# The tail of a fused attention and density kernel: four endings moved to GpSimd, and one term of each sum written to PSUM by ScalarE

## The chip, the cores and the metric

The kernel runs on one core of a Trainium2 chip. Its engines are TensorE (PE in the profile), VectorE (DVE), ScalarE (ACT), GpSimd (POOL) and SyncE (SP, which issues DMAs). Each takes its own instructions in the order in which they were written and waits on semaphores for the others. The metric is the device time of one execution in microseconds.

## What is computed

The input has 8 images of 192 channels and 64 x 64 positions, in float32. After a group norm and an attention over positions, whose result is added to the input, comes a second group norm and a small per-channel network of four layers (1-3-3-3-1), evaluated at the normalized value minus and plus one half:

```
lower = _logits_cumulative(xr - 0.5, ms, bs, fs)
upper = _logits_cumulative(xr + 0.5, ms, bs, fs)
sign = -jnp.sign(lower + upper)
likelihood = jnp.abs(sigmoid(sign * upper) - sigmoid(sign * lower))
x = x + jnp.maximum(likelihood, 1e-06)
```

Each layer is `logits = softplus(m) @ logits + b`, and all but the last add `tanh(f) * tanh(logits)`. The network is called the density below.

## The kernel before

**Stages.** The attention of the 8 images runs as one stream of 1,024 steps. An image's density needs the norm over all of its attention output, so it runs beside the attention of the next image; that of the last image has nothing beside it and is the tail of the kernel.

**Units.** A density is cut into 12 units (`Unit`, L908): two column halves c, three channel groups g, and s = 0, 1 for lower and upper, in that order. A unit works on 128 x 1024 tiles, and a pair s = 0, 1 is followed by an `ending` (L1173). In the tail a unit goes thus:

- three tanh of the input on ACT (`tanh0`, L1015), called u;
- three sums of layer 1 on PE (`product`, L983), each four terms: one in x and three in the u, with diagonal matrices as weights and two matmuls of 512 columns per term, added up in one of four PSUM tiles (`banks`: b0, b1, sc_tail, mx_tail[...]). `tanh1` (L996, ACT) and `gate1` (L1006, DVE) read the sum, and the gate gives the tile back;
- layer 2: three rows, each a scaled copy on ACT (`scaled`, L1040) and two additions on DVE (`more`), a tanh (`tanh`, L1030) and a gate (`gate`). `more` and `gate` are written by `stt`, L1047;
- layer 3: one scaled copy and two additions.

**Endings.** While attention runs, an ending is cut into half-tile pieces for POOL (`total`, `difference`, `masked`, L1195 to L1218), with the tanh and the sign on ACT (L1202, L1204); ahead of each piece a small memset (`pause`, L1163) waits for the last DVE operation but one, so that the piece falls beside the reduce that reads PSUM. In the tail an ending is `alone` (L1220): sum (L1227), difference (L1239) and mask (L1240) on DVE, two whole tanh on ACT (L1233). Both close with an Abs on ACT (L1249) and a `store` on DVE (L1254) with two DMAs. Units of earlier images also leave two pieces each for POOL (`plain`, L1072 and L1078).

**What sets the order.** The program writes its instructions in ticks. In each, `density_step` (L1120) gives every engine a credit, and units (up to four in the tail) issue their next operations while credit lasts, at the costs of `COST` (L866), if their inputs were issued in an earlier tick, a PSUM tile is free and enough of the 17 buffers are left for older units (`need`, L1094). Other work is put on a list by tick (`at`, `later`). In the tail the rate is `RATE` = 4.15 (L1426). `pool_step` (L1158) issues one piece per tick.

Of the kernel before, what the change touches and what calls it, by code (L numbers as in the profile page):

```python
# [10 lines left out]
AF = mybir.ActivationFunctionType  # L11
# [6 lines left out]
def kernel(  # L18
# [43 lines left out]
    nc = tc.nc  # L62

    B, C, H, W = x.shape
# [12 lines left out]
    last = B * IMG  # L77
# [40 lines left out]
    for i in range(3):  # L118
        t = xin.tile([128, 3, P], F32, tag=f"xi{i}", name=f"xi{i}")
# [58 lines left out]
    for i in range(2):  # L178
        nc.vector.tensor_reduce(
            out=bb[i], in_=ident[:, 64 * i + CR : 64 * i + 64 : 32], axis=AX.X, op=ALU.add  # L180
# [6 lines left out]
    for s in range(2):  # L187
        p = slice(R * s, R * s + R)
# [45 lines left out]
    for src, dst, at, n in (  # L234
# [4 lines left out]
        for s in range(2):  # L239
            nc.sync.dma_start(  # L240
                out=dst[R * s : R * s + R, :, at : at + n],
# [85 lines left out]
    now = [0]  # L327
# [538 lines left out]
    COST = {"DVE": 1.22, "ACT": 1.23, "TANH": 1.05, "PE": 6.95}  # L866
    diag = []
    banks = deque()
    lower2 = mm.rearrange("p g n -> p (g n)")[:, 0:36].rearrange("p (s g i) -> p s g i", s=4, g=3)

    def diagonals(g, t):
# [36 lines left out]
    class Unit:  # L908
# [3 lines left out]
        def __init__(self, b, c, g, s):  # L912
            self.key = b, c, g, s
            self.at = {}
            self.buf = {}
            self.todo = {"DVE": deque(), "ACT": deque(), "PE": deque()}
            self.left = {"l": 6, "t": 9, "u": 0, "z": 1, "p": 1}
            self.held = {"l": 0, "t": 0, "u": 0, "z": 0, "p": 0}
            self.on_pe = b == B - 1
            add = self.add  # L920
            if self.on_pe:

                self.left.update(t=3, u=3, p=0)
                for i in range(3):
                    add("ACT", ("u", 0, i), [], self.tanh0, makes="u")
                for i in range(3):
                    add(
                        "PE", ("sum", i), [("u", 0, j) for j in range(3)], self.product,
                        frees=[("u", 0, j) for j in range(3)] if i == 2 else [],
                    )  # L930
                    add("ACT", ("l", 1, i), [("sum", i)], self.tanh1, makes="l")
                for i in range(3):
                    add("DVE", ("gate", 1, i), [("l", 1, i)], self.gate1)
            else:
                for i in range(3):
                    add("ACT", ("t", 0, i), [], self.tanh0, makes="t")
                    add("ACT", ("l", 1, i), [], self.linear, makes="l")
                for i in range(3):
                    for j in range(3):
                        add(  # L940
                            "DVE", ("mix", i, j), [("t", 0, j), ("l", 1, i)], self.mix,
                            frees=[("t", 0, j)] if i == 2 else [],
                        )
                    add("ACT", ("t", 1, i), [("mix", i, 2)], self.tanh, makes="t")
                for i in range(3):
                    add("DVE", ("gate", 1, i), [("t", 1, i)], self.gate, frees=[("t", 1, i)])
            for i in range(3):
                add("ACT", ("l", 2, i), [("gate", 1, 0)], self.scaled, makes="l")
                for j in (1, 2):
                    add("DVE", ("add", 2, i, j), [("gate", 1, j), ("l", 2, i)], self.more)  # L950
                add("ACT", ("t", 2, i), [("add", 2, i, 2)], self.tanh, makes="t")
            for i in range(3):
                add("DVE", ("gate", 2, i), [("t", 2, i)], self.gate, frees=[("t", 2, i)])
            add("ACT", ("l", 3, 0), [("gate", 2, 0)], self.scaled, makes="z")
            add("DVE", ("add", 3, 0, 1), [("gate", 2, 1), ("l", 3, 0)], self.more)
            if self.on_pe:
                add("DVE", ("add", 3, 0, 2), [("gate", 2, 2), ("l", 3, 0)], self.more)
            else:

                add("ACT", ("p", 3, 2), [("gate", 2, 2), ("add", 3, 0, 1)], self.plain, makes="p")  # L960

        def add(self, eng, name, after, fn, makes=None, frees=()):
            self.todo[eng].append((name, after, fn, makes, frees))
# [15 lines left out]
        def src(self):  # L979
            b, c, g, s = self.key  # L980
            return xc[b, c][:, g, :]

        def product(self, k):  # L983
            g, i = self.key[2], k[1]
            out = self.buf[k] = banks.popleft()
            for n, src in enumerate([self.src()] + [self.buf["u", 0, j] for j in range(3)]):
                for h in range(2):
                    nc.tensor.matmul(  # L988
                        out[:, h, :], lhsT=diag[g][:, 3 * i + n - 1 if n else 9 + i, :],
                        rhs=src[:, h * F : h * F + F], start=n == 0, stop=n == 3,  # L990
                    )

        def tanh1(self, k):
            b, c, g, s = self.key
# [6 lines left out]
        def gate1(self, k):  # L1001

            g, i = self.key[2], k[2]
            dst = self.buf["l", 1, i].rearrange("p (h n) -> p h n", h=2)
            src = self.buf.pop(("sum", i))
            nc.vector.scalar_tensor_tensor(  # L1006
                dst, dst, tf[:, g, 3 + i : 4 + i], src, ALU.mult, ALU.add
            )
            banks.append(src)

        def tanh0(self, k):
            b, c, g, s = self.key
# [81 lines left out]
        def need(self):  # L1094
            most = dict(self.left, t=max(0, min(self.left["t"], 1 - self.held["t"])))
            if ("add", 2, 2, 2) not in self.at:

                most.update(z=0, p=0)
            return sum(most.values())

        def step(self, eng, t, older):
            todo = self.todo[eng]
            while todo and credit[eng] > 0:
                name, after, fn, makes, frees = todo[0]
                if any(self.at.get(a, t) >= t for a in after if eng != "DVE" or a[0] in "ltu"):
                    return
                if eng == "PE" and not banks:
                    return
                if makes and len(bufs) <= sum(u.need() for u in older) + len(endings):
                    return  # L1110
                todo.popleft()
                if makes:
                    self.take(name, makes)
                fn(name)
                self.at[name] = t
                for k in frees:
                    self.give(k)
                credit[eng] -= COST["TANH" if name[0] == "t" and name[1] else eng]
# [39 lines left out]
    def pool_step():  # L1158


        if pieces:
            if len(recent) == 2:
                inst = nc.gpsimd.memset(pause, 0.0)  # L1163
                tc.add_manual_dep(
                    inst.ins, recent[0].ins.name,
                    mybir.DependencyInfo(
                        mybir.DependencyClass.Sync, mybir.DependencyReason.DATA
                    ),
                    reason="beside the reduce",
                )  # L1170
            pieces.popleft()()

    def ending(b, c, g):  # L1173

# [8 lines left out]
        def begin():  # L1183
            if not bufs:
                later(1, begin)
                return
            endings.pop()
            cell["s"] = bufs.pop(0)
            if now[0] < last - 12:
                for h in range(2):  # L1190
                    pieces.append(lambda h=h: total(h))
            else:
                alone()
# [26 lines left out]
        def alone():  # L1220

            s = cell["s"]
            parts = halves if (b, c, g) == (B - 1, 1, 2) else [slice(0, 2 * F)]

            def first():
                for n in parts:
                    nc.vector.tensor_tensor(s[:, n], z[0][:, n], z[1][:, n], ALU.add)  # L1227
                later(1, second, 0.0, 2.1)

            def second():  # L1230
                for n in parts:
                    for i in range(2):
                        nc.scalar.activation(z[i][:, n], z[i][:, n], AF.Tanh, scale=0.5)  # L1233
                later(1, third, 2.5)

            def third():
                for n in parts:
                    y = z[0][:, n]
                    nc.vector.tensor_tensor(y, z[1][:, n], y, ALU.subtract)  # L1239
                    nc.vector.scalar_tensor_tensor(y, s[:, n], 0.0, y, ALU.not_equal, ALU.mult)  # L1240
                bufs.extend((s, z[1]))
                later(1, lambda: size(parts), 0.0, 1.1)
                later(2, lambda: store(parts), 1.3)

            later(1, first, 1.25)
# [177 lines left out]
    homes[:] = [(turns[1], [0, 0])]  # L1423
    while due or units or jobs or loads:

        work_off(t, RATE if (B - 1, 1) in norms else 1.3)  # L1426
        t += 1
# [1 line left out]

# [36 lines left out]
```

## Time and profile before

| | |
|---|---|
| median of 3 runs | 4800.04 us (4797.65 to 4801.9) |
| the profiled execution | 4801.53 us |
| its span, first to last instruction | 4799.7 us |
| busy over the span | PE 97%, DVE 87%, ACT 67%, POOL 18% |
| in 4473 to 4527 us (54 us) | PE 34.37, DVE 51.23, ACT 35.47, POOL 9.05 us; clock 0.79 |
| in 4527 to 4588 us (61 us) | PE 56.06, DVE 45.60, ACT 37.69, POOL 0 us; clock 1.00 |
| a PE record of L988 | 592 ns, a new one every 0.43 us at full clock; two records per matmul |

Durations include the time in which an operation's end overlaps the start of the next one, so back-to-back starts are closer together than durations suggest: L1030 lasts 1.05 us and is followed 0.95 us later. "idle before <- releaser" in a timeline is how long the engine stood before the instruction, and what released it. A window row gives, for each engine, its busy time in that stretch and the number of instructions, and at the end the granted TensorE clock (1.00 is full speed).

### The profile page before, as it was taken

How to read it: one execution, taken by the hardware profiler on the slowest of the kernel's cores; microseconds unless marked ns; L12 is line 12 of the kernel's file. 1: busy time of each engine (PE TensorE's matmuls, PEld its weight loads, DVE VectorE, ACT ScalarE, POOL GpSimd, SP SyncE). 2: the span in 40 equal slices, each digit the busy share in tenths (PEclk: the TensorE clock that was granted, in tenths of full speed). 3: DMA queues.
4: the chain of work that ended last, by engine and by line, in shares of the span. 5: the costliest groups of instructions: out<-in, count | busy, mean ns of one | idle time of the engine just before them, and what ended most of it. 6: DMA issues, size and time to landing. Idle time of an engine off the chain costs nothing.

```text
span 4799.7 us, 69014 instructions
## 1 busy us (share of the span) xinstructions
PE 4653.4 (97%) x28432; PEld 3440.0 (72%) x28432; DVE 4179.0 (87%) x4289; ACT 3196.8 (67%) x3665; POOL 856.3 (18%) x842
## 2 busy tenths in 40 slices
PE   7999999999999999999999999999999999999686
PEld 5777777777777777777777777777777777777332
DVE  5433359999999999999999999999999999998788
ACT  2333246777677767776777767777777777777675
POOL 0000001222122211221211221122222132222000
PEclk9999999999999999999999999999999999999898
DMA  2101020111110111010110111101111101000000
GB/s 58 41 18 29 18 48 14 35 28 29 42 27 25 37 39 34 27 44 9 36 46 26 33 40 33 32 19 33 36 38 33 34 13 27 10 12 16 9 13 13
DMA packets 109328, 138.60 MB, mean 29 GB/s; under 512 B 17106, under 2 KB 82132, under 8 KB 109012
## 3 DMA queue, kind: packets, MB, share of 16 engines
q1 hardware_dynamic: 107776, 133.81, 11.4%
q8 instruction: 223, 3.65, 0.3%
q14 instruction: 93, 0.76, 0.1%
q10 hardware_dynamic: 1236, 0.37, 0.0%
HBM read 100.58 MB, written 29.36 MB: 27 GB/s over the span
## 4 chain that ended last, share of the span: by engine, by line
PE 86%; DVE 7%; ACT 5%; issue 1%; DMA 0%; POOL 0%; ACTq 0%; SPq 0%; DVEq 0%; POOLq 0%
PE b L795 53%; PE sc L780 20%; PE b L669 4%; DVE d L1047 4%; PE b L988 2%; PE b L620 2%; DVE rm L716 1%; ACT d L1015 1%; ACT e L784 1%; PE mx_tail L988 1%; PE sc_tail L988 1%; PE b L828 1%; PE mx L708 1%; ACT d L1040 1%; PE b L745 0%
## 5 line engine op out<-in xcount | busy, mean ns | idle before, releaser
L795 PEld LDWEIGHTS b<-v,e 128*128 128x128 f32 x16384 | 2651.8, 190 | 776.9 <-issue 771.6
L795 PE MATMUL b<-v,e 128*128 128x193 f32 x16384 | 2955.7, 334 | 0.0
L784 ACT ACTIVATE e<-sc 128x1024 f32<-128x1024 f32 x1024 | 1045.9, 1021 | 1353.4 <-PE mx L708 1330.8
L716 DVE TENSOR_REDUCE rm<-mx 128x1 f32<-128x1024 f32 x1002 | 1222.3, 1220 | 481.4 <-PE mx L708 472.7
L780 PE MATMUL sc<-q,k 25*128 25x512 f32 x4096 | 1155.1, 640 | 24.2 <-ACT e L784 22.9
L708 PE MATMUL mx<-k,q 24*128 24x512 f32 x4008 | 1130.4, 640 | 0.6 <-DVE rm L716 0.6
L1047 DVE SCALAR_TENSOR_TENSOR d<-d,lc,d 128x1024 f32<-128x1024 f32 x756 | 986.1, 1314 | 12.2
L1047 DVE SCALAR_TENSOR_TENSOR d<-d,wsp,d 128x1024 f32<-128x1024 f32 x684 | 883.3, 1292 | 53.1 <-ACT d L1040 44.7
L1047 DVE SCALAR_TENSOR_TENSOR d<-d,tf,d 128x1024 f32<-128x1024 f32 x540 | 687.5, 1292 | 0.4 <-ACT d L1030 0.4
L1163 POOL MEMSET pause<- 128x1 f32 x408 | 40.0, 98 | 3613.2 <-DVE d L1047 3613.2
L1030 ACT ACTIVATE d<-d 128x1024 f32<-128x1024 f32 x540 | 568.2, 1054 | 42.6 <-DVE d L1047 40.8
L780 PEld LDWEIGHTS sc<-q,k 25*128 25x128 f32 x4096 | 306.2, 183 | 252.4 <-issue 175.8
L1040 ACT ACTIVATE d<-d,cb,wsp 128x1024 f32<-128x1024 f32 x348 | 429.9, 1236 | 4.3 <-DVE d L1047 3.3
L1015 ACT ACTIVATE d<-xc,bn,wn 128x1024 f32<-128x1024 f32 x288 | 354.0, 1236 | 7.7 <-issue 5.9
L1078 POOL TENSOR_TENSOR d<-d,d 128x512 f32<-128x512 f32 x168 | 331.8, 1975 | 47.7 <-ACT d L1072 46.6
L1024 ACT ACTIVATE d<-xc,bn,wn 128x1024 f32<-128x1024 f32 x252 | 311.8, 1237 | 0.0
L708 PEld LDWEIGHTS mx<-k,q 24*128 24x128 f32 x4008 | 299.8, 183 | 7.3 <-DVE rm L716 6.7
L1198 POOL TENSOR_TENSOR d<-d,d 128x512 f32<-128x512 f32 x80 | 173.0, 2163 | 0.0
L1210 POOL TENSOR_TENSOR d<-d,d 128x512 f32<-128x512 f32 x80 | 163.2, 2040 | 0.5 <-issue 0.5
L1218 POOL TENSOR_TENSOR d<-d,d 128x512 f32<-128x512 f32 x80 | 157.6, 1970 | 2.5 <-POOL pause L1163 0.9
L669 PE MATMUL b<-wv,xi 64*128 64x192 f32 x1344 | 139.5, 340 | 0.0
L669 PEld LDWEIGHTS b<-wv,xi 64*128 64x128 f32 x1344 | 106.5, 186 | 25.4 <-issue 21.5
(155 smaller groups left out, 2303.9 us busy)
## 6 DMA issues: line engine op xcount, KB each, us to landing
xi<-in_x_dram SPq DMA_DIRECT2D x280, 192.0 KB, 3.5
xc<-in_x_dram SPq DMA_DIRECT2D x64, 384.0 KB, 7.1
out_dram<-xc SPq DMA_DIRECT2D x94, 256.0 KB, 3.1
q<-qd SPq DMA_DIRECT2D x128, 128.0 KB, 2.7
k<-kq SPq DMA_DIRECT2D x64, 64.0 KB, 1.9
qd<-kq SPq DMA_DIRECT2D x64, 64.0 KB, 2.0
d<-in_x_dram SPq DMA_DIRECT2D x16, 192.0 KB, 4.1
out_dram<-xc SPq DMA_DIRECT2D x4, 128.0 KB
```

The source lines that it names most:

```text
L669: nc.tensor.matmul(pv[:, s, 0:C], lhsT=t[p, g, k * 128 : k * 128 + 128] if g < 3 else one_row[p], rhs=wf["v", b][p, g, :] if g < 3 else wf ...
L708: nc.tensor.matmul(sc[:, s, :], lhsT=tile_of(qt[b, n // 2], n, j)[r], rhs=kt[b][r, u : u + F], start=True, stop=True,)
L716: nc.vector.tensor_reduce(out=rowmax[b, n][:, j, k : k + 1], in_=sc, axis=AX.XY, op=ALU.max)
L780: nc.tensor.matmul(sc[:, s, :], lhsT=kt[b][r, k : k + 128], rhs=qt[b, n // 2][r, :, u : u + 256], start=True, stop=True,)
L784: return lambda: nc.scalar.activation(e, sc, AF.Exp)
L795: nc.tensor.matmul(a[:, j, 0 : C + 1], lhsT=e[:, s, j * 128 : j * 128 + 128], rhs=v[:, s, p % 4, :], start=p == 0 and s == 0 and j % 2 == ...
L1015: nc.scalar.activation(self.buf[k], self.src(), AF.Tanh, bias=bn[:, s, g, 0, i : i + 1], scale=wn[:, g, 0, i : i + 1],)
L1024: nc.scalar.activation(self.buf[k], self.src(), AF.Identity, bias=bn[:, s, g, 1, i : i + 1], scale=wn[:, g, 1, i : i + 1],)
L1030: nc.scalar.activation(self.buf[k], self.buf["l", k[1], k[2]], AF.Tanh)
L1040: nc.scalar.activation(self.buf[k], self.buf["l", n - 1, 0], AF.Identity, bias=offset, scale=wsp[:, g, w : w + 1],)
L1047: nc.vector.scalar_tensor_tensor(dst, src, factor, dst, ALU.mult, ALU.add)
L1078: return nc.gpsimd.tensor_tensor(z[:, n], z[:, n], dst[:, n], ALU.add)
```

## The change

1. `fill`: for the second and third sum of a unit in the tail, ACT writes the term in x (a scaled copy of x) into the PSUM tile, if a product has been in that tile before (`full`). The product then leaves its two matmuls in x out and adds onto what is there. The tanh of a sum is written behind the next sum instead of behind its own.
2. Endings of the last image with 3c + g < 4, four of its six, are cut into POOL pieces. A piece is issued in `gate1`, with its pause waiting for the DVE operation before the gate; `pool_step` issues none while the oldest unit is one of the tail's.
3. Orders: the tail's rate is 2.5 for 4.15; a tail unit whose third sum is not yet issued reserves its missing u and four buffers more (`need`); an ending of an earlier image first issues the pieces that are left.

The core of the diff (line numbers of the changed kernel: fill L998, product L1014, `tanh1` L1025, `gate1` L1035, pause L1201):

```
                 for i in range(3):
+                    after = [("u", 0, j) for j in range(3)]
+                    if i:
+                        add("ACT", ("fill", i), [("sum", 0)], self.fill)
+                        after.append(("fill", i))
                     add(
-                        "PE", ("sum", i), [("u", 0, j) for j in range(3)], self.product,
+                        "PE", ("sum", i), after, self.product,
...
-                    add("ACT", ("l", 1, i), [("sum", i)], self.tanh1, makes="l")
+                    if i:
+                        add("ACT", ("l", 1, i - 1), [("sum", i - 1)], self.tanh1, makes="l")
+                add("ACT", ("l", 1, 2), [("sum", 2)], self.tanh1, makes="l")
...
+        def fill(self, k):
+            b, c, g, s = self.key
+            i = k[1]
+            if id(banks[0]) in full:
+                out = self.buf["sum", i] = banks.popleft()
+                nc.scalar.activation(
+                    out, self.src().rearrange("p (h n) -> p h n", h=2), AF.Copy,
+                    scale=norms[b, 1][0][:, g, 1, i : i + 1],
+                )
...
             for n, src in enumerate([self.src()] + [self.buf["u", 0, j] for j in range(3)]):
+                if n == 0 and filled:
+                    continue
...
+            if filled:
+                credit["PE"] += 1.7
...
-            nc.vector.scalar_tensor_tensor(
+            recent.append(nc.vector.scalar_tensor_tensor(
                 dst, dst, tf[:, g, 3 + i : 4 + i], src, ALU.mult, ALU.add
-            )
+            ))
             banks.append(src)
+            if pieces and len(recent) == 2:
+                piece()
...
+            if self.on_pe and ("sum", 2) not in self.at:
+                return most["u"] + 4
...
-        if pieces:
+        if pieces and not (units and units[0].on_pe):
+            piece()
...
-            if now[0] < last - 12:
+            if now[0] < last - 12 or b == B - 1 and 3 * c + g < 4:
...
             def first():
+                while pieces and b < B - 1:
+                    piece()
...
-        work_off(t, RATE if (B - 1, 1) in norms else 1.3)
+        work_off(t, 2.5 if (B - 1, 1) in norms else 1.3)
```

## What was predicted

> **What bounds the kernel.** I read the page's chain by line first, to find which part of it the change can touch.
>
> ```profile
> PE 86%; DVE 7%; ACT 5%; issue 1%; DMA 0%; POOL 0%; ACTq 0%; SPq 0%; DVEq 0%; POOLq 0%
> PE b L795 53%; PE sc L780 20%; PE b L669 4%; DVE d L1047 4%; PE b L988 2%; PE b L620 2%; DVE rm L716 1%; ACT d L1015 1%; ACT e L784 1%; PE mx_tail L988 1%; PE sc_tail L988 1%; PE b L828 1%; PE mx L708 1%; ACT d L1040 1%; PE b L745 0%
> ```
>
> The attention stages (L795, L780) keep their instructions. What changes begins at L988, the tail: the stretch from 4470 us, where the last image's density starts, to 4799.7. At most some 330 us are in play. Next the tail by windows, each from one unit's first layer-2 addition to that of the unit two later (a pair s=0,1 with its ending).
>
> ```profile
> core 0: us, PE busy (x) PEld busy (x) DVE busy (x) ACT busy (x) POOL busy (x), PEclk, DMA share, GB/s
> 4634.52:4679.81 45.29, 41.74 (x97) 18.07 (x96) 39.25 (x34) 31.25 (x30) 0.00 (x0) 1.00 0.05 12
> 4679.81:4725.10 45.29, 41.73 (x97) 18.07 (x96) 39.24 (x33) 31.25 (x30) 0.00 (x0) 1.00 0.05 12
> 4770.38:4799.70 29.32, 0.00 (x0) 0.00 (x0) 19.03 (x20) 10.12 (x12) 0.00 (x0) 0.52 0.08 18
> ```
>
> A pair takes 45.3 us; PE is busy for 41.7, DVE 39.25, ACT 31.25, POOL not at all. The last 29.3 us hold no product. The chain in such a pair:
>
> ```profile
> 4679.45 12.28 PE b L988 x28
> 4691.73 6.88 PE sc_tail L988 x16
> 4698.64 1.11 ACT d L996
> 4699.76 1.13 ACT d L1040
> 4700.88 1.14 ACT d L1015
> ```
>
> PE and its wait for the next unit's tanh set the pace. DVE's own waits, in its timeline:
>
> ```profile
> 4634.52 2.60 DVE L1047 SCALAR_TENSOR_TENSOR d<-d,wsp,d 128x1024 f32<-128x1024 f32 x2
> 4639.38 2.60 DVE L1047 SCALAR_TENSOR_TENSOR d<-d,wsp,d 128x1024 f32<-128x1024 f32 x2 [2.25 <-ACT d L1040]
> 4641.90 1.27 DVE L1006 SCALAR_TENSOR_TENSOR d<-d,tf,sc_tail 128x1024 f32<-128x1024 f32 x1
> 4644.24 2.60 DVE L1047 SCALAR_TENSOR_TENSOR d<-d,wsp,d 128x1024 f32<-128x1024 f32 x2 [1.07 <-ACT d L1040]
> ```
>
> From two additions to the next two is 4.85 us: ACT's next row product stands behind a tanh that needs the first two. It is a round trip, and no engine is full in it.
>
> **What the change takes and adds.** A product is 16 records of 0.43 us, 6.87. The order of the changed kernel has 22 fills (every second and third product but the first unit's, since a bank must have been written before), so PE sheds 4 records, 1.72 us, 22 times: 37.8 us, 6.9 of a pair's 41.7. ACT gains 22 fills. No ACT write into PSUM stands in the trace. Nearest are the scaled copy L1072 (1.13 us, SBUF to SBUF) and the PSUM-reading L996 (1.11); starts follow each other about 0.1 sooner, so 1.05. Ends: 0.95 and 1.24 (the two-pointer L1015). Two stand on a unit's path, so the ends are worth -0.2 and +0.4 a unit where nothing covers them, about -2 and +4 us over the tail.
>
> Four endings lose three DVE operations each (starts 1.14, 1.26 and 1.14 us apart: 3.54), 14.2 in all. POOL gains six half pieces and a pause per ending, ACT six half activations (0.63 us each by L1202 and L1204, 0.53 apart: 3.2) for two whole tanh (1.9): +1.3. The stores and their DMAs stay, later and far from the end; SP's queue has nothing behind them that anyone waits for.
>
> The planner's edits (rate 2.5, the smaller reserve of buffers, pieces issued in the gate) cost no instruction of their own; they act through the order, which I take as it stands, with the buffers that an ending now holds for longer in it.
>
> What is a piece worth? Ends: nothing, where DVE waits anyway, and its whole duration. DVE's and then POOL's timeline in a stretch beside the reduce, which reads PSUM, and then all pieces of that line (shortest, median, longest ns):
>
> ```profile
> 4157.16 2.47 DVE L1047 SCALAR_TENSOR_TENSOR d<-d,tf,d 128x1024 f32<-128x1024 f32 x2
> 4159.70 1.23 DVE L716 TENSOR_REDUCE rm<-mx 128x1 f32<-128x1024 f32 x1
> 4160.84 2.60 DVE L1047 SCALAR_TENSOR_TENSOR d<-d,wsp,d 128x1024 f32<-128x1024 f32 x2
> ```
>
> ```profile
> 4158.55 0.10 POOL L1163 MEMSET pause<- 128x1 f32 x1 [13.67 <-DVE d L1047]
> 4158.80 1.97 POOL L1078 TENSOR_TENSOR d<-d,d 128x512 f32<-128x512 f32 x1
> ```
>
> ```profile
> L1078 POOL TENSOR_TENSOR d<-d,d x168: 1260/2148/2389, 759.6 to 4524.2; 128x512 f32<-128x512 f32 x168
> ```
>
> By the median row a piece is 2.15 us, and beside a gate of 1.2 it would reach 0.95 into the next DVE operation plus its start. The Trainium skill (SBUF — State Buffer, "Who interferes with whom") says a VectorE instruction with two SBUF inputs and a GpSimd one exclude each other for the whole instruction, while one with a single SBUF input does not contend. The rows bear it out: the piece at 4158.80 ends 1.14 us after the addition that ends at 4159.63, the reduce is not lengthened, and the row's shortest is 1.26. So most of the 2.15 is waiting. L1006 reads one operand from PSUM, so I take 1.26 us, starting 0.25 after the gate: 0.3 us of delay to the next operation. By the rule 24 pieces cost 7 us, by the row 23 or more, against 14.2 shed. I take the rule's 0.3.
>
> **The pair, walked.** I follow the four queues in the changed order with the durations above. X is the unit before, A and B the pair; zero is X's first layer-2 addition. DVE: additions to 2.5; round trip, next at 4.85 (2.3 idle); round trip, next at 9.70 (2.3 idle), to 12.22. ACT's fill for A's second product stands behind those round trips, at 9.56 to 10.7, though PE is done with the first before: PE idles about 3 us, then ends A's products at 15.9 and 21.1. DVE goes on: two gates 14.6, PSUM gate 15.8, piece 16.1, gate and two additions 19.8, PSUM gate 21.0. The last piece of an ending ends at 21.33; Abs waits for it at the head of ACT's queue (behind it the tanh of A's third sum), is done at 22.4, and the store, after one more piece, starts at 22.7 (1.7 idle). Store and PSUM gate to 25.05, additions, round trip, 29.90 (2.3 idle), to 32.4; PSUM gate 33.6. A's last row leaves ACT at 35.1, behind the second pair of fills (1.5 idle). Additions 37.7, two gates 40.1, PSUM gate and piece 41.6, gate and two additions 45.3, PSUM gate and piece **46.8**. So 36.7 busy and 10.1 waiting, for 39.25 and 6.05: PE has been relieved, but the round trips now stand bare, and the period is **1.5 us longer**. PE's second batch ends at 41.4, with slack.
>
> PE's new 3 us gaps can cool it. The Trainium skill (TensorE: Matmul & The Clock Gate, "What's actually happening") gives an idle window of about 3.4 us; the trace shows half speed already after 3.25 (8 records in 5.10 us, PE's timeline below) and not after 2.75 (at 4588.82, 12 in 5.42).
>
> ```profile
> 4502.62 5.10 PE L988 MATMUL mx_tail<-d,v 128*128 128x512 f32 x8 [3.25 <-ACT d L1015]
> 4521.96 3.78 PE L988 MATMUL mx_tail<-d,v 128*128 128x512 f32 x4 [14.24 <-ACT d L1015]
> ```
>
> Cold, a gap costs about 1.6 us; the slack at A (1.2) and B (some 3) takes nearly all. By the page's rule nothing, by the row perhaps 0.5 a pair.
>
> The pair with the last pieces and a DVE ending comes to 48.1 by the same walk: its first half as above, then the three DVE operations again; fills leave at 35.3 and 37.5 and PE's last product ends at 45.7. Three pairs of +1.5 and one of +2.8: **7.3 us lost**.
>
> **The head.** Before, the first bank of the second unit waited 14.24 us (row above) for its tanh while DVE finished the image before. In the new order two tanh of that unit stand earlier in ACT's queue (about 4510.4 for 4520.7), so that sum is done near 4516.7 instead of 4525.7. DVE, full until then, passes its first ending addition at 4524.9 (4526.5), gains on the gaps of 3.3, 3.9, 2.3 and 3.8 us that follow before, and starts the first walked pair at about 4581.0 where the trace has 4588.4. **7.4 us won.** The before interval from 4588.43 to 4634.52 is 46.1, not 45.3, which gives back 0.8.
>
> Sum: -7.4 + 7.3 - 0.8 = -0.9 us; the last 29.3 us are the same instructions. The profiled execution is 4801.5 with 1.8 outside its span, so 4800.6; the median of the runs is 1.5 lower: **4799**.
>
> **Rivals.** *The round trips close up.* If half of the 10.1 us of waiting goes (an Abs that doesn't hold ACT back, queues that settle into another phase), a pair is near 42 and four win 12 us more: about 4786, -0.3%. For it: PE falls to 34.8 and POOL pairs have 36.7 of DVE. Against: every wait named has an ACT instruction behind another.
> *The pieces bite.* If the PSUM gate excludes POOL, or a piece takes its 2.15 us, each delays DVE by 0.95 for 0.3: 24 times 0.65, 15.6 us, 4815, slower. It decides from 0.74 us of delay a piece (4809.6).
> **Numbers.** Forecast within 0.2% (9.6 us, about what a measurement can tell from no change): 0.50. Closing up: 0.28. Pieces: 0.22. The forecast's own spread, +-2 a pair and 3 in the head, is 4790 to 4808; the range reaches into both rivals, 4783 to 4814.
>
> **What would show it.** PE busy near 35 in a pair with gaps near 3 us before the second products; DVE idle about 10; L1006 at 1.27 us and the operation after it late by 0.3; Abs waiting for POOL; first walked pair at 4581. Pairs at 43 or below, or pieces of 2 us beside L1006, would make it wrong.

## The result, and the profile after

The changed kernel takes 4802.43 us (median of 12 runs, 4800.21 to 4804.61) where the kernel before, run beside it, takes 4799.75 (12 runs, 4797.54 to 4801.9): a ratio of 1.0005 with a 95% interval of 0.9998 to 1.0013. That is within the 0.2% of no change. The profiled execution's span is 4800.9 us, for 4799.7.

Little moved in the total, much inside. In short: before, PE's products and their wait for the next tanh set the pace of the tail, 45.3 us a pair; with PE relieved, the alternation of DVE and ACT sets it, and a pair takes 46 to 47.5 us (the last one 50). First the chain of waits of the changed kernel, by engine and by line:

```profile
PE 83%; DVE 8%; ACT 6%; issue 2%; DMA 0%; POOL 0%; SPq 0%; ACTq 0%; DVEq 0%; POOLq 0%
PE b L795 53%; PE sc L780 20%; DVE d L1079 5%; PE b L669 4%; PE b L620 2%; DVE rm L716 1%; ACT e L784 1%; ACT d L1047 1%; PE b L828 1%; ACT d L1072 1%; PE mx L708 1%; PE b L1014 1%; ACT d L1062 1%; PE mx_tail L1014 1%; PE b L745 0%
```

The three entries for the products (L988 before, L1014 now) had 4% of the span, now the two that are left have 2%; the additions and gates that `stt` writes (L1047 before, L1079 now) went from 4% to 5%, and the row product L1072 and the tanh L1062 stand in the list with 1% each. In the stretch of the four pairs alone the turn is clear: the chain between 4588 and 4770 us of the kernel before is 76% PE, 14% ACT and 7% DVE, that between 4581 and 4772 us of the changed kernel 27% PE, 26% ACT and 40% DVE. The windows of the pairs, from first layer-2 addition to first layer-2 addition, and then the end (columns as in the windows of the kernel before; the third pair, left out, takes 46.17 us):

```profile
4581.10:4628.03 46.93, 37.25 (x82) 15.56 (x81) 36.45 (x30) 36.65 (x38) 8.13 (x13) 0.96 0.04 11
4628.03:4675.49 47.46, 39.54 (x81) 16.30 (x80) 36.40 (x30) 36.62 (x37) 8.03 (x13) 0.89 0.04 12
...
4721.66:4771.90 50.24, 37.39 (x74) 14.85 (x72) 41.08 (x35) 34.40 (x32) 3.12 (x5) 0.86 0.08 21
4771.90:4800.90 29.00, 0.00 (x0) 0.00 (x0) 19.04 (x20) 10.12 (x12) 0.00 (x0) 0.53 0.08 18
```

A pair with POOL pieces has DVE 36.4 us busy where it had 39.25, and is nevertheless longer, 46 to 47.5 us for 45.3. No engine fills it. What DVE stood for after 4580 us is in the view of waits, first of the kernel before, then of the changed one (total, times, longest):

```profile
DVE d L1047 <- ACT d L1040: 23.5, 14, 2.3
```

```profile
DVE d L1079 <- ACT d L1072: 34.8, 17, 2.3
DVE xc L1295 <- ACT d L1290: 4.8, 3, 1.9
```

With the smaller entries the waits rose from 27.8 to 44.5 us, 11.3 of it on the row product, that is on the round trips. The balance from the first walked pair to the end: DVE's busy time fell from 177.1 us (158.1 in the four pairs and 19.0 after) to 169.2, and its other time rose from 34.1 to 50.6. So this stretch is 8.5 us longer, and the head is 7.3 us shorter (4581.10 for 4588.43): +1.2, the difference of the spans. Of the 7.3 us, 1.2 are not the tail's: in this execution attention ended that much earlier (first product of the tail at 4469.67 for 4470.91).

### The profile page after: what moved, and what is told of

It reads as the page before. It is cut to its first block, busy times and chain, and to the rows that moved or that the text cites. A ratio compares the mean times of both kernels' runs of the same rounds, so it can differ in the third digit from the quotient of the medians.

```text
span 4800.9 us, 68965 instructions
## 1 busy us (share of the span) xinstructions
PE 4630.9 (96%) x28344; PEld 3424.8 (71%) x28344; DVE 4166.9 (87%) x4277; ACT 3224.6 (67%) x3703; POOL 888.1 (18%) x890
## 4 chain that ended last, share of the span: by engine, by line
PE 83%; DVE 8%; ACT 6%; issue 2%; DMA 0%; POOL 0%; SPq 0%; ACTq 0%; DVEq 0%; POOLq 0%
PE b L795 53%; PE sc L780 20%; DVE d L1079 5%; PE b L669 4%; PE b L620 2%; DVE rm L716 1%; ACT e L784 1%; ACT d L1047 1%; PE b L828 1%; ACT d L1072 1%; PE mx L708 1%; PE b L1014 1%; ACT d L1062 1%; PE mx_tail L1014 1%; PE b L745 0%
## 5 line engine op out<-in xcount | busy, mean ns | idle before, releaser
L780 PE MATMUL sc<-q,k 25*128 25x512 f32 x4096 | 1155.2, 640 | 24.3 <-ACT e L784 22.9
L1079 DVE SCALAR_TENSOR_TENSOR d<-d,lc,d 128x1024 f32<-128x1024 f32 x756 | 987.5, 1316 | 12.2
L1079 DVE SCALAR_TENSOR_TENSOR d<-d,wsp,d 128x1024 f32<-128x1024 f32 x684 | 884.4, 1294 | 70.0 <-ACT d L1072 61.6
L1201 POOL MEMSET pause<- 128x1 f32 x432 | 42.6, 99 | 3797.8 <-DVE d L1079 3797.8
L1079 DVE SCALAR_TENSOR_TENSOR d<-d,tf,d 128x1024 f32<-128x1024 f32 x540 | 686.6, 1291 | 0.4 <-ACT d L1062 0.4
L1062 ACT ACTIVATE d<-d 128x1024 f32<-128x1024 f32 x540 | 568.4, 1054 | 48.5 <-DVE d L1079 46.6
L1072 ACT ACTIVATE d<-d,cb,wsp 128x1024 f32<-128x1024 f32 x348 | 430.0, 1236 | 4.2 <-DVE d L1079 3.2
L1047 ACT ACTIVATE d<-xc,bn,wn 128x1024 f32<-128x1024 f32 x288 | 354.9, 1237 | 7.7 <-issue 5.9
L1110 POOL TENSOR_TENSOR d<-d,d 128x512 f32<-128x512 f32 x168 | 331.0, 1971 | 47.5 <-ACT d L1104 46.5
L1236 POOL TENSOR_TENSOR d<-d,d 128x512 f32<-128x512 f32 x88 | 183.4, 2084 | 0.3 <-issue 0.2
L1248 POOL TENSOR_TENSOR d<-d,d 128x512 f32<-128x512 f32 x88 | 173.5, 1972 | 0.5 <-issue 0.5
L1256 POOL TENSOR_TENSOR d<-d,d 128x512 f32<-128x512 f32 x88 | 168.0, 1909 | 2.6 <-POOL pause L1201 0.9
L1014 PE MATMUL b<-d,v 128*128 128x512 f32 x216 | 105.5, 640 | 32.6 <-ACT d L1047 18.0
```

The costliest lines, as they stand in the source:

```text
L780: nc.tensor.matmul(sc[:, s, :], lhsT=kt[b][r, k : k + 128], rhs=qt[b, n // 2][r, :, u : u + 256], start=True, stop=True,)
L1047: nc.scalar.activation(self.buf[k], self.src(), AF.Tanh, bias=bn[:, s, g, 0, i : i + 1], scale=wn[:, g, 0, i : i + 1],)
L1062: nc.scalar.activation(self.buf[k], self.buf["l", k[1], k[2]], AF.Tanh)
L1072: nc.scalar.activation(self.buf[k], self.buf["l", n - 1, 0], AF.Identity, bias=offset, scale=wsp[:, g, w : w + 1],)
L1079: nc.vector.scalar_tensor_tensor(dst, src, factor, dst, ALU.mult, ALU.add)
L1110: return nc.gpsimd.tensor_tensor(z[:, n], z[:, n], dst[:, n], ALU.add)
```

## Experiments

All were timed beside the kernel before (medians 4799.76 to 4799.96 us), 4 to 21 runs each. The last column is taken from the traces, one execution each: from the first product of the tail to the end of the span. It leaves out where attention ended, which differs by up to 4.4 us between the profiled executions. Its differences to the kernel before agree with those of the medians within 2 us.

| kernel | median, us | ratio to before, 95% interval | tail in the trace, us |
|---|---|---|---|
| before | 4799.75 | | 328.8 |
| changed | 4802.43 | 1.0005 (0.9998 to 1.0013) | 331.2 |
| e1 fills, endings on DVE | 4793.81 | 0.9987 (0.9981 to 0.9994) | 323.1 |
| e2 POOL endings, no fills | 4800.69 | 1.0000 (0.9991 to 1.0008) | 331.2 |
| e3 no term in x at all | 4797.17 | 0.9994 (0.9986 to 1.0002) | 325.0 |
| e4 changed, rows ahead | 4786.07 | 0.9968 (0.9956 to 0.9981) | 315.9 |
| e5 e1, rows ahead | 4786.31 | 0.9972 (0.9961 to 0.9983) | 314.5 |
| e6 before, rows ahead | 4782.69 | 0.9965 (0.9952 to 0.9979) | 312.1 |
| e7 changed, no Abs | 4804.06 | 1.0007 (0.9999 to 1.0015) | 331.6 |
| e8 changed, short pieces | 4799.16 | 0.9998 (0.9990 to 1.0007) | 328.4 |
| e9 changed order, pieces on DVE | 4810.41 | 1.0019 (1.0010 to 1.0028) | 338.7 |
| e10 order of e1, endings on POOL | 4806.48 | 1.0014 (1.0007 to 1.0020) | 334.3 |
| e11 e5 with two buffers more | 4770.40 | 0.9937 (0.9924 to 0.9951) | 300.9 |
| e12 e6 with two buffers more | 4757.39 | 0.9913 (0.9899 to 0.9926) | 286.4 |

My theory at the start: the changed kernel's tail is bound by round trips between DVE and ACT, so what PE and DVE shed is lost in waits. The first rival: the POOL pieces cost by themselves.

### The two halves of the change: e1 and e2

e1 keeps the fills and gives the endings back to DVE:

```diff
-            if now[0] < last - 12 or b == B - 1 and 3 * c + g < 4:
+            if now[0] < last - 12:
```

> The changed kernel with all six tail endings on DVE again; fills and planner edits stay. Theory (order and round trips between DVE and ACT set the pace of the tail): three DVE operations a pair come back, 3.5 us, the wait of Abs and store for POOL (2 us) and the pieces' delay (1 us) go; a pair stays at 46 to 48 us and the kernel within 6 us of both, 4796 to 4806. Rival (the fills win by relieving PE, and the POOL pieces eat it up): clearly faster than both, 4790 or less. Rival (the fills themselves are what costs, the pieces win): 4810 or more.

e2 keeps the POOL endings and writes no fill:

```diff
-            if id(banks[0]) in full:
+            if False and id(banks[0]) in full:
```

> The changed kernel without fills: PE does all four terms again; POOL endings and planner edits stay. Theory: PE is the bound again, 41.2 us of products a pair plus its wait for a tanh, so relief of DVE is worth nothing: pairs of 45 to 46 us, and only the head's lead can show, so 4793 to 4802. Rival (pieces cost more than they take from DVE): 4806 or more. Rival (the DVE relief carries the change): 4788 or less.

Measured: e1 4793.81, below its range; e2 4800.69, within it, though not for its reason: I expected PE to be the bound there, and the chain of e2 between 4580 and 4770 us is 42% DVE, 27% ACT and 22% PE. Alone, the fills with the planner's edits win 6 us; no run has those edits with neither fills nor POOL endings, so what they give by themselves is not shown. A pair of e1 takes 44.6 us (4631.75 to 4676.33) with PE busy for 36.8: of the 6.9 us taken off PE, 0.7 arrives, and the chain of e1's pairs is 12% PE and 59% DVE. The POOL endings win nothing alone, and on top of the fills they take all of it back: 8.6 us between e1 and the changed kernel. By the traces they shorten the head (from the first product to the first walked pair: 115.3 us in e1, 111.4 in the changed kernel) and lengthen the rest (207.7 and 219.8). The reason shows when the same stretch of both is laid side by side. DVE's timeline in the second unit of a pair of e1:

```profile
4654.99 1.22 DVE L1268 TENSOR_TENSOR d<-d,d 128x1024 f32<-128x1024 f32 x1
4657.33 2.60 DVE L1079 SCALAR_TENSOR_TENSOR d<-d,wsp,d 128x1024 f32<-128x1024 f32 x2 [1.12 <-ACT d L1072]
4659.85 1.22 DVE L1280 TENSOR_TENSOR d<-d,d 128x1024 f32<-128x1024 f32 x1
4661.10 1.22 DVE L1281 SCALAR_TENSOR_TENSOR d<-d,d 128x1024 f32<-128x1024 f32 x1
4662.34 2.60 DVE L1079 SCALAR_TENSOR_TENSOR d<-d,wsp,d 128x1024 f32<-128x1024 f32 x2
```

And in the changed kernel, around the same unit:

```profile
4651.23 1.23 DVE L1295 SCALAR_TENSOR_TENSOR xc<-d,xc 128x1024 f32<-128x1024 f32 x1 [1.92 <-ACT d L1290]
...
4659.18 2.60 DVE L1079 SCALAR_TENSOR_TENSOR d<-d,wsp,d 128x1024 f32<-128x1024 f32 x2 [2.25 <-ACT d L1072]
4661.69 1.28 DVE L1035 SCALAR_TENSOR_TENSOR d<-d,tf,b 128x1024 f32<-128x1024 f32 x1
4664.33 2.61 DVE L1079 SCALAR_TENSOR_TENSOR d<-d,wsp,d 128x1024 f32<-128x1024 f32 x2 [1.36 <-ACT d L1072]
```

A round trip takes 4.85 us from additions to additions whatever stands in it. In e1 the ending's sum (L1268) fills half of one and its other two operations all of the next: there is no wait before 4662.34. An operation in such a gap costs nothing, so taking it away wins nothing there.

Why it even loses shows on PE, in the first unit of the same pair. PE's timeline of e1 and then of the changed kernel:

```profile
4630.86 5.31 PE L1014 MATMUL sc_tail<-d,v 128*128 128x512 f32 x12
4637.62 5.42 PE L1014 MATMUL mx_tail<-d,v 128*128 128x512 f32 x12 [1.45 <-ACT mx_tail L998]
```

```profile
4634.24 3.78 PE L1014 MATMUL sc_tail<-d,v 128*128 128x512 f32 x4 [3.71 <-ACT d L1047]
4639.03 7.75 PE L1014 MATMUL mx_tail<-d,v 128*128 128x512 f32 x12 [1.01 <-ACT mx_tail L998]
```

In the changed order the third u (L1047) stands in ACT's queue behind the first tanh of layer 2, which waits for DVE. PE stands 3.71 us for it, comes back at half speed (3.78 us for four records, 1.88 at full speed), and the fill of the next sum goes out one round trip later. Counted from the unit's first addition (4631.75 in e1, 4628.03 here), the product into mx_tail ends 11.3 us on in e1 and 18.8 us on here, and the next unit begins its layer 2 after 20.7 and 26.3 us. So part of the price is the order that came with the POOL pieces. e9 and e10 below take the two apart.

### Is PE's work on the path: e3

22 sums leave out their term in x: neither the fill nor the matmuls are there, and the order of everything else is that of the changed kernel.

```diff
             if id(banks[0]) in full:
-                out = self.buf["sum", i] = banks.popleft()
+                self.buf["sum", i] = banks.popleft()
+                return
...
-                        rhs=src[:, h * F : h * F + F], start=n == 0, stop=n == 3,
+                        rhs=src[:, h * F : h * F + F], start=n == (1 if filled else 0), stop=n == 3,
```

> Leaves out the term in x in the 22 sums that are filled: no fill on ACT and no matmul for it, so 22 fewer ACT operations of 1.1 us and PE as in the changed kernel; every other instruction and its order are those of the changed kernel. Theory: DVE's loop through the round trips is the bound, and of the fills only the two ahead of the first unit's last layer-2 row lie on it (about 1.5 us a pair), plus the late end of the products in the last pair (2 to 3 us): 4790 to 4796. Rival (the fills' ACT time and PE's wait for them are the bound): pairs fall to 42 or below, 4785 or less. Rival (fills cost nothing): 4801 to 4803.

Measured: 4797.17 (interval 0.9986 to 1.0002), just above the range; the tail in the trace is 6.2 us shorter than the changed kernel's. So in this order all 22 fills together cost 5 to 6 us, some 0.3 us each where one takes 1.04 from start to start (the intervals of the two ratios just touch). And with neither the fills nor the 88 PE records (37.8 us) the kernel is as fast as before within the interval: in the changed order hardly any of PE's relief arrives.

### What the pieces cost: e7 and e8

e7 leaves out the Abs of the four POOL endings, e8 works on 64 of the 512 columns of each piece; both keep the order.

```diff
-                later(1, size, 0.0, 1.1)
+                later(1, (lambda: None) if b == B - 1 else size, 0.0, 1.1)
```

```diff
+        def short(h):
+            n = halves[h]
+            return slice(n.start, n.start + 64) if b == B - 1 else n
...
-            n = halves[h]
+            n = short(h)
```

> The changed kernel leaving out the Abs of the four POOL endings (the store adds the difference of those four without its absolute value); order of all other instructions is the same. It takes away ScalarE's wait for the last piece and the store's wait of 1.4 to 1.9 us for Abs. Theory: four times some 1.5 us of VectorE's wait, 4794 to 4799. Rival (the waits only move into the next round trip): no change, 4802.

> The changed kernel with the tail's 24 POOL pieces on 64 of their 512 columns (the rest of the four endings is left out); the order is the same. It takes away the delay of 0.15 to 0.2 us that a piece puts on the next VectorE operation, and about 0.9 us of the wait for each last piece. Theory: 24 times 0.15 to 0.2 us and four times up to 0.9, less what falls into waits: 3 to 8 us, 4794 to 4799. Rival (pieces bite: VectorE and POOL exclude each other): over 12 us, 4790 or below. Rival (nothing of it is on the path): 4802.

e7: 4804.06, no gain; my theory of the Abs falls. DVE's timeline at the store shows why (the stretch of the fence above, where the store waited 1.92 us):

```profile
4652.89 2.32 DVE L1295 SCALAR_TENSOR_TENSOR xc<-d,xc 128x1024 f32<-128x1024 f32 x1 [0.32 <-POOL pause L1201]
4656.38 1.28 DVE L1035 SCALAR_TENSOR_TENSOR d<-d,tf,b 128x1024 f32<-128x1024 f32 x1 [1.17 <-ACT d L1025]
```

The store starts 1.6 us after the gate ahead of it (4651.28) instead of 3.2, but takes 2.32 us instead of 1.23, because the first piece of the next ending (4652.86 to 4654.12) runs on POOL beside it. Then the next gate waits for its tanh, whose sum PE ends only at 4655.2. From gate to gate it is 5.10 us, and 5.09 with the Abs: here the late sum was behind the Abs all the time. At the store of the next pair no sum is late, and the longer store alone takes back what the Abs gave (3.86 us from gate to gate, for 3.87).

e8: 4799.16, 3.3 us below the changed kernel, at the lower edge of what I expected from the delays and the waits for the last piece; the intervals of the two ratios overlap, and the tails in the trace say 2.8. Even that is not the pieces' own alone: in the pair that gained most (44.77 us from 4628.51, where the changed kernel has 47.46) PE also returned to full speed earlier (last section). So the pieces as such cost about 3 us or less, not the 8.6 between e1 and the changed kernel, and the rival that they bite falls.

### Order or engine: e9 and e10

e9 keeps the changed order and gives the 24 pieces to DVE, each at its gate; e10 keeps the order of e1 and gives the same four endings to POOL.

```diff
+        half = nc.vector if b == B - 1 else nc.gpsimd
...
-            return nc.gpsimd.tensor_tensor(cell["s"][:, n], z[0][:, n], z[1][:, n], ALU.add)
+            return half.tensor_tensor(cell["s"][:, n], z[0][:, n], z[1][:, n], ALU.add)
```

(and the same for the two other pieces); e10, on e1:

```diff
+            on_pool = b == B - 1 and 3 * c + g < 4
...
-                    nc.vector.tensor_tensor(s[:, n], z[0][:, n], z[1][:, n], ALU.add)
+                    (nc.gpsimd if on_pool else nc.vector).tensor_tensor(s[:, n], z[0][:, n], z[1][:, n], ALU.add)
...
+                    if on_pool:
+                        nc.scalar.activation(s[:, n], s[:, n], AF.Sign)
...
+                    if on_pool:
+                        nc.gpsimd.tensor_tensor(y, z[1][:, n], y, ALU.subtract)
+                        nc.gpsimd.tensor_tensor(y, y, s[:, n], ALU.mult)
+                        continue
```

> The order of the changed kernel kept on every engine, with the 24 half pieces of its four endings given to VectorE, each at the place of its gate. VectorE gets 24 times some 0.65 us, 15.6 us, and the pieces no longer wait for POOL. Theory (the order costs, not the engine): all but a few of these fall into VectorE's waits or take the place of waiting for POOL's last piece (four times up to 1.9 us), so 4802 to 4810. Rival (POOL relieves VectorE as meant, and the order hides it): 4814 to 4818.

> The order of e1_fills_only kept, with the operations of its first four endings given to POOL as half pieces at their places (two tanh and a sign in halves on ScalarE, no pause). VectorE sheds 14.2 us. Theory (in this order the VectorE operations stood in waits): nothing is won, and ScalarE waits for POOL's pieces, two waits of 1 to 3 us per ending of which part reaches VectorE: 4793 to 4803. Rival (VectorE's work bounds the tail): 14 us less, 4780 to 4785.

Measured: 4810.41 and 4806.48. By the tails of the traces, the order of e1 has 323.1 us with DVE and 334.3 with POOL, the changed order 338.7 with DVE and 331.2 with POOL. So POOL does relieve DVE in the changed order: 7.5 us, half of the 15.6 that the pieces take on DVE; neither my theory nor its rival for e9 had half. But the changed order is itself 15.6 us dearer when DVE does the work in both (1.4 of that because 24 halves of 0.65 us are more than 12 wholes of 1.18). The medians say the same: 8.0 for the engine, 16.6 for the order. ACT's six half activations per ending, for two whole tanh in e1, are in the price of the order too, and no run takes them out; the changed kernel's chain between 4581 and 4772 us has none of them. What the change won by the engine it paid twice over by the order, of which the late third u above is the part that I can show.

e10 came out above my range. I had counted ScalarE's waits for POOL (one of 1.02 us per ending, at the Abs) and not that in this order the pieces fall beside additions of three SBUF tiles. Both suffer; DVE's and POOL's timeline:

```profile
4654.48 3.59 DVE L1079 SCALAR_TENSOR_TENSOR d<-d,wsp,d 128x1024 f32<-128x1024 f32 x2
4666.56 3.35 DVE L1079 SCALAR_TENSOR_TENSOR d<-d,wsp,d 128x1024 f32<-128x1024 f32 x2 [2.74 <-ACT d L1072]
```

```profile
4662.81 2.13 POOL L1287 TENSOR_TENSOR d<-d,d 128x512 f32<-128x512 f32 x1
```

Two additions take 3.35 to 3.59 us instead of 2.60, and a piece up to 2.25 instead of 1.26. They do not run at once: at the first of these lines the first addition ends at 4655.87, the piece that started in it (at 4654.74) ends 1.12 us later, and the second addition 1.08 us after that. Three such pairs of additions are 2.6 of the 3.0 us by which this stretch is longer than in e1 (15.4 us to 4669.84, for 12.4 from 4652.47). The rest fits ACT, which has six half activations ahead of its next tanh where e1 has two whole ones. The changed kernel's choice of place, beside the gate that reads PSUM, avoids this.

### The round trips themselves: e4, e5, e6

In the tail ACT's row product of layer 2 is written ahead of the tanh of the row before, on the changed kernel (e4), on e1 (e5) and on the kernel before (e6):

```diff
-                add("ACT", ("t", 2, i), [("add", 2, i, 2)], self.tanh, makes="t")
+                if not self.on_pe:
+                    add("ACT", ("t", 2, i), [("add", 2, i, 2)], self.tanh, makes="t")
+                elif i:
+                    add("ACT", ("t", 2, i - 1), [("add", 2, i - 1, 2)], self.tanh, makes="t")
+            if self.on_pe:
+                add("ACT", ("t", 2, 2), [("add", 2, 2, 2)], self.tanh, makes="t")
```

> The changed kernel with one more edit: in the tail's units ACT's product for the next layer-2 row stands ahead of the tanh of the row before, so that DVE need not wait for that tanh. Theory: four waits of 2.3 us a pair fall to about half a microsecond or nothing, and two more in the last 29 us; pairs near 41 to 43 us (busy: DVE 36.7, ACT 37, PE 35), so 4772 to 4786. Rival (pieces, fills or PE bound the pair, the round trips only fill up time that is idle anyway): 4797 to 4805.

> Rows ahead of the tanh as in e4_rows_ahead, and the six endings of the tail on VectorE as in e1_fills_only; the fills stay. Theory (a POOL ending cost time in the changed kernel because the VectorE operations that it replaced had stood in the round-trip waits): with the round trips gone the VectorE operations no longer fall into waits, so undoing the POOL endings brings little here, within 4 us of e4_rows_ahead: 4782 to 4790. Rival (the pieces cost by themselves: delay of VectorE, Abs that waits): undoing them wins what it won without the reordering, some 8 us: 4778.

> The kernel before with rows ahead of the tanh, nothing else. Theory: in the kernel before TensorE's 41.2 us of records and its wait for the next unit's u set the pair, so of the round trips only those of the last unit (two of 2.3 us) and some of the waits for u go: 4785 to 4797, less than the 14 us won on the changed kernel. Rival (round trips bounded the kernel before as well, the fills are beside the point): as much as there, 4786 or below.

Measured: 4786.07, 4786.31, 4782.69. e4 and e5 are equal, so with the round trips gone it no longer matters which engine does the endings: the theory held there. The kernel before gains 17.1 us by the same edit, which is the rival's number, and with it the whole change is worth nothing: e4 and e5 stand 3.4 and 3.6 us above e6, within the intervals. The waits of DVE in e6, after 4580 us:

```profile
DVE d L1011 <- ACT d L1001: 14.9, 8, 3.2
DVE d L1052 <- ACT d L1045: 0.6, 2, 0.3
```

The 23.5 us on the row product have become 0.6; what is left is waiting for sums. A pair takes 43.4 us (two pairs from 4540.19 to 4626.88), 41.2 of them PE records.

The rival's reason does not hold, though. DVE's waits for the row product fell by 22.9 us and a pair by 1.9, because in neither kernel do the pairs hang on DVE: the chain of e6 between 4583 and 4756 us is 84% PE, 15% ACT and less than 0.1% DVE. Where PE waits, the chain runs from the end of its products through a tanh of the sum, row products and a u, as in the kernel before:

```profile
4667.23 1.11 ACT d L1001
4668.34 2.26 ACT d L1045 x2
4670.60 1.14 ACT d L1020
```

In the new order one u is already there, PE can take up its term, and the wait is 1.2 us for 1.8 and comes less often. After 4530 us PE's waits fall from 18.3 to 8.3. The end wins the rest: from PE's last product to the end of the span it is 27.0 us for 33.2, and there, behind the last products, the round trips of the last unit did stand on the path. Together that is 16.2 of the 16.7 us between the tails.

### What is late next: e11 and e12

Two SBUF tiles of attention, free by then, are added to the 17 buffers when the tail starts, on e5 (e11) and on e6 (e12):

```diff
             banks.append(t)
+        for i in range(2):
+            e = work.tile([128, 2, F], F32, tag="e", bufs=2, name=f"e_tail{i}")
+            bufs.append(e.rearrange("p h n -> p (h n)"))
```

> e5_rows_nopool with two buffers more in the tail (19 for 17), which lets a unit's u be written earlier. What waits there is VectorE, for a tanh of a sum that is late (waits of 2.7 to 3.9 us on L1030, some 10 us a pair). Theory (the sums are late because their u or fills stand late in ScalarE's queue for want of buffers): half of these waits or more go, four times 4 us: 4765 to 4776. Rival (ScalarE's queue order alone): no change, 4784 to 4788.

> e6_before_rows with the same two buffers more; no fills, TensorE has 41.2 us of records a pair. Theory (there TensorE bounds the pair, 43.4 us of which 41.2 are records): at most 2 us a pair, 4774 to 4783, and more than e11_rows_bufs. Rival (fills are worth nothing in any order): equal to e11_rows_bufs within 3 us.

Measured: 4770.40, in its range, and 4757.39, far below its range; the rival that both would be equal falls too. A window of e12:

```profile
4580.00:4625.00 45.00, 45.00 (x106) 19.95 (x105) 44.68 (x38) 36.59 (x35) 0.00 (x0) 1.00 0.05 12
```

PE is busy in every microsecond at full clock, and so it is in the next two stretches of 45 us. I had counted only what a pair could win. Half came from the head: PE's waits between the tail's first product and 4530 us fell from 19.4 (e6) to 6.6, after that from 8.3 to 0, and the last product ends at 4731.4 instead of 4753.9. e12 is faster than both kernels by 42 us or more, without any part of the change. In e11 PE stands still for 41.2 us, and its records take 20.9 us longer than at full speed, against 6.6 and 4.6 in e12: 50.9 us more, where the fills take 37.8 off it. e11 also has the rate 2.5, the other reserve of buffers and the changed place of the tanh of a sum. Whether e12 with the fills alone would be faster still was not tried and stays open.

## Why the prediction was right, and where it was not

**The head** was right in its mechanism and partly lucky in its number. Two u stand further ahead in ACT's queue, and the sum that waited for them is done at 4516.0 (4516.7 forecast); the first walked pair, forecast at 4581.0, starts at 4581.10. But 1.2 us of that is attention's earlier end, which no part of my account gives; the tail's first product lies anywhere from 4468.1 to 4472.5 in these traces, so it may be chance. Counted from the first product the head is 6.1 us shorter, not 7.4. DVE was not full until its first ending addition either (4523.66, for 4524.9): it waited 2.42 us there for a POOL piece.

**The pairs** were right in mechanism, and three of the four in number: "PE has been relieved, but the round trips now stand bare" is what the chains and DVE's waits show. PE's gap of near 3 us stands at another place than I had it: 3.71 us ahead of the first sum's last term, which waits for the third u, and 1.0 to 2.8 us ahead of the second product. Walked 46.8 each; measured 46.93, 47.46 and 46.17, together 140.56 for 140.4. The mis-sized term is the last pair, "three pairs of +1.5 and one of +2.8": it took 50.24 us, not 48.1. The third u of its second unit stands behind a tanh and an Abs that wait for DVE, and what follows on PE starts late and slow (PE's timeline):

```profile
4754.48 3.78 PE L1014 MATMUL b<-d,v 128*128 128x512 f32 x4 [4.50 <-ACT d L1047]
4758.06 6.25 PE L1014 MATMUL sc_tail<-d,v 128*128 128x512 f32 x12
```

I let PE end 45.7 us into the pair; it ended at 47.8 (4769.45), and the last gate waits 2.63 us for it. The four pairs gave +8.85 us where my terms made 7.3 - 0.8 = 6.5, the head -7.33 for -7.4 and the end -0.32 for 0, so the span grew by 1.2 where I had -0.9; without attention's earlier end it is 2.4, and by the medians 2.7.

**The pieces** are 1.26 to 1.28 us beside the gate, so the value chosen was right and the row's median of 2.15 would have been wrong. The operation after it was late by 0.15 (1.43 for 1.28) or 0.2 us (2.81 for 2.60 in two additions; once 2.91), for 0.3. 24 times that would be 4 us; e8 says about 3 in all with the waits for the last pieces. The page quoted there (SBUF — State Buffer, "Who interferes with whom" in the Trainium skill) says "for the whole instruction" of VectorE's two-port modes, and of two SBUF inputs only that they contend; that they too wait out the whole instruction is what e10 and the store of e7 show.

**The fill** starts 1.04 us after the one before, taken as 1.05.

**PE's speed after a gap** I gave 0 to 0.5 us a pair, since slack would take it. There are more and longer gaps than I walked (39 us after 4580 us, 15 before), and PE's records in the tail are 25.7 us longer than at 0.43 us each (8.5 before). Most of it is hidden, as e3 shows, which has 28.1 us of it and is 5 us faster. But in the second pair the chain of waits goes through the product of 7.75 us shown above: 2.3 us over the 5.42 of e1, and that pair is the longest of the three. My walk met 46.8 there partly because its wait for the Abs stood where in fact the late sum did (e7).

**The bound before and the lever.** "PE and its wait for the next unit's tanh set the pace" holds for the kernel before: the chain of its pairs is 76% PE, the u that PE waits for stand behind a tanh of PE's own sum (L996 and L1015 in the chain of the prediction), and e12, where PE no longer stands still after 4530 us, is the fastest. What I had too small is the worth of the order. The rival "the round trips close up" rightly named the lever, but I gave it to the change, which does not touch it. And I took the order of the planner as given; e11 and e12 show that with two buffers more it places the u so much earlier that the tail is 14 and 26 us shorter.

## What to carry to other kernels

Relief of the engine that sets the pace is worth only the distance to the next loop: here 6.9 us off PE's share of a pair brought 0.7 (e1). Where two engines answer each other and neither is full, as DVE and ACT do in that next loop, work on either is free as long as it fits the gap: taking it off one of them wins nothing, and the move can lose what the old order hid. First look at which instruction stands at the head of the queue when an engine idles, and ask whether an independent one behind it could go ahead: here six lines of order and two idle tiles won 42 us where less work on the two busiest engines won none. Test a move between engines with the order held fixed on both sides, or the price of the order is taken for that of the engine.

## What the hardware showed beyond that

A GpSimd piece that starts while a VectorE gate reads PSUM takes its 1.26 to 1.28 us, and the gate keeps 1.28; beside a VectorE operation on SBUF alone both get longer (3.35 to 3.59 for 2.60, 2.13 to 2.25 for 1.26, and the store 2.32 for 1.23). ScalarE's scaled copy into PSUM takes 1.10 us, its copy from SBUF to SBUF with a scale and an offset per channel 1.23.

TensorE's half speed after a gap did not follow from the gap's length. The same place in e8, where the pieces are short and the gap is 3.36 us for 3.71:

```profile
4634.52 3.55 PE L1014 MATMUL sc_tail<-d,v 128*128 128x512 f32 x4 [3.36 <-ACT d L1047]
4639.31 5.42 PE L1014 MATMUL mx_tail<-d,v 128*128 128x512 f32 x12 [1.24 <-ACT mx_tail L998]
```

The four records are as slow (3.55 us), but the next twelve are at full speed (5.42 us); in the changed kernel they took 7.75. After the same gap of 3.71 us at 4681.70 they took 5.42 again, and at 4587.42 the four records after 3.67 us were at full speed and the twelve after the next gap of 2.81 were not (7.11 us). So half speed came after a gap of 3.36 us as well, and how soon and how long it follows differs from one equal gap to the next. The Trainium skill (TensorE: Matmul & The Clock Gate, "What's actually happening"), which the prediction quotes for its idle window of about 3.4 us, also says that the window is free-running. An idle window that does not start with the gap would give such differences, but no run here tested it by itself.
